# Recurrence steps folded into the input projection, and three re-orderings in the attention loop

## The chip, the cores and the metric

The kernel runs on one core of one Trainium2 chip. The metric is the device time of one execution in microseconds (us). TensorE (PE in the profile) multiplies matrices into the accumulation memory PSUM[...]; VectorE (DVE) and ScalarE (ACT) read and write PSUM and the on-chip memory SBUF; GpSimd (POOL) works on SBUF alone; transfers are issued from the SP and POOL queues. Each engine works through its own instructions in program order and waits on semaphores where it needs another's result. All data here is fp32.

## The reference, cut to what matters

```python
x = L0_attn_x                                   # (2, 2048, 256)
# 1. layernorm, then a tanh recurrence along the sequence, added back
xi = layernorm(x) @ Wi.T + bi
h_t = tanh(xi_t + h_{t-1} @ Wh.T + bh)          # for t in 0..2047, h_{-1} = 0
x = x + h
# 2. layernorm, then attention with experts, added back: 8 heads of 64, 5 experts, 2 of them taken
xn = layernorm(x)
q, k = xn @ Wq, xn @ Wk
gl_v, gl_o = xn @ Ws, xn @ Wd                   # gates, per head and expert
xv = einsum('btd,edk->btek', xn, Wv)            # experts' values
v = einsum('bthe,btek->bhtk', top2(gl_v) * sigmoid(gl_v), xv)
attn = softmax(q @ k.T / 8) @ v
out = x + einsum('bthe,bthk,ekd->btd', top2mask(gl_o), attn, Wo)
```

## The kernel before

**The recurrence.** The sequence of 2048 is cut into 128 pieces of 16 positions; all pieces advance together, so a step is one product with `Wh` over 2 x 128 columns. Since a piece needs the state at the end of the one before it, the recurrence is run twice: run "a" starts every piece from zero at position 3 (`SKIP`) and keeps only the last states (`ends`); run "b" starts from these and keeps all states (`hs`). `compare` (L502) checks that both give the same last states to within 4 x 2^-23; if not, a flag makes the kernel do everything again in a slow form.

The stage ahead of the runs works on 16 chunks `c`. `measure` takes statistics on DVE, `turn_in` (L290) normalizes on POOL and transposes on PE, `project_in` (L301) multiplies by `Wi` (eight PE instructions of 256 columns, an fp32 product being two instructions) and ACT writes `xi` with the bias added. The chunks' order on PE is written out at L322: transposes of chunk c+1, then the product of chunk c. When all sixteen are done, `run("a", ...)` (L375, `step` at L355) follows: each step has per batch four products of 128 columns, an addition of `xi` on DVE and a tanh on ACT.

**The attention.** There are 64 *units*, one for each batch, head and quarter of 512 queries. A unit takes eight score tiles, each of 128 partitions x 2 x 512. The loop at L1154 goes over *steps* T, four for each unit (`U_T`), two score tiles a step. PSUM holds two score tiles (two banks each), two banks for everything else (`misc`), one for the products (tag "o") and one for the sums (tag "d").

A unit is spread over ten steps and more: in four steps its scores are made, ACT copies each tile to SBUF (`stage`, L648) and DVE folds it into a running maximum (`largest`, L653). Then `turn_max`, `reduce_max` and `spread_max` make the row maxima. Five steps after the scores (`LAG` - 1) its tiles have the maximum taken off (`subtract`, L701: the first two tiles of a unit on DVE, the other six on POOL), ACT takes the exponential (L708), PE multiplies by the values (`products`, L711), a DMA on POOL's queue adds tiles in pairs (`fold`, L728), and PE sums them (`sums`). `take` (L751) then takes the products out of bank "o": ACT copies one half, DVE adds the other.

The order on each engine in a step is the program's: at most one `take` and an exponential; scores; `stage`; the table `between`; the two `largest`; the `subtract`s and folds; the table `before`; products; sums; an exponential; the tables `first_behind` and `behind`. Work of other stages (keys and queries of later heads, the second batch's layernorm and gates, experts' values, the output projection `PLACES`) is put into these tables under a step number.

A step in which the first two tiles of a unit have their maximum taken off is called *fresh*; these are the steps with T mod 4 = 1. On DVE a fresh step goes: `largest` of the second tile, `subtract`, `largest` of the first tile, `subtract`. A score tile's banks are free for PE again when both `stage` and `largest` have read them. A unit's last products are made in a fresh step; `take` follows at the head of the step after it (L1158 to L1162), ahead of everything else on ACT.

**The first head.** In steps 0 to 5 `first_experts` (L594) makes the experts' values of the first batch, three chunks a step (16 PE instructions each), using bank "d" for odd chunks and `misc` for even ones. `mix` and `mix_sum` (L613, L626) weigh them with the gates in four parts, on DVE, at the end of steps 3, 5, 6 and 7. The experts' values of the second batch (`experts`, L586) are made during head 5, in steps 81 to 111, two chunks in every four steps; head 8 fetches them from step 120 on. The second batch's layernorm is turned and its logits are made in steps 55 to 89 (`turn_late`, `logits_late`); its gates follow in steps 91 to 121.

Of the kernel before, what the change touches and what calls it, by code (L numbers as in the profile page):

```python
# [14 lines left out]
P = 128  # L15
# [5 lines left out]
def pass_over(  # L21
# [237 lines left out]

    S = NCH  # L260
    NS = P
    NEWTON = 3


# [8 lines left out]

    with tile_pool(name="prep", bufs=3) as pp, tile_pool(
        name="lna", bufs=3
    ) as lnp, tile_pool(name="ps_xi", bufs=3, space=PSUM) as ps_xi, tile_pool(
        name="ps_t", bufs=3, space=PSUM
    ) as ps_t, tc.manual_schedule():
        norm_of, turned = {}, {}

        def measure(c0, n):
            mv = pp.tile([P, n * B, 2], F32, tag=f"mv{n}", name=f"mva{c0}")
            for c in range(c0, c0 + n):
                for b in range(B):
                    stats(lnp, mv[:, (c - c0) * B + b, :], xt[c][:, b, :], f"a{c}_{b}")
            neg, y = scales(lnp, mv, n * B, f"a{c0}")
            for c in range(c0, c0 + n):
                norm_of[c] = neg, y, (c - c0) * B

        def turn_in(c):  # L290
            neg, y, k = norm_of.pop(c)
            xn = pp.tile([P, B, D], F32, tag="xn", bufs=2, name=f"xn{c}")
            tp = ps_t.tile([P, KC, B, P], F32, tag="tp", name=f"tpa{c}")
            for b in range(B):
                normalize(xn[:, b, :], xt[c][:, b, :], neg, y, k + b)
                for kc in range(KC):
                    nc.tensor.transpose(tp[:, kc, b, :], xn[:, b, kc * P : (kc + 1) * P], ident)
            turned[c] = pp.tile([P, KC, B, P], F32, tag="xnT", bufs=2, name=f"xnT{c}")
            nc.scalar.copy(turned[c], tp)

        def project_in(c):  # L301
            xnT = turned.pop(c)
            for mc in range(KC):
                px = ps_xi.tile([P, B, P], F32, tag="px", name=f"px{c}_{mc}")
                for kc in range(KC):
                    nc.tensor.matmul(  # L306
                        px.rearrange("p b n -> p (b n)"),
                        lhsT=wi[:, kc, mc * P : (mc + 1) * P],
                        rhs=xnT[:, kc].rearrange("p b n -> p (b n)"),
                        start=kc == 0,  # L310
                        stop=kc == KC - 1,
                    )
                nc.scalar.activation(xi[:, mc, c], px, AF.Identity, bias=bsum[:, mc : mc + 1])

        groups, c0 = [], 0
        for n in (1, 1, 2, 3, 4, 5):
            groups.append((c0, n))
            c0 += n
        assert c0 == NCH
        measure(*groups.pop(0))  # L320
        nc.vector.tensor_tensor(bsum, bias[:, 0, :], bias[:, 1, :], ALU.add)
        for c in range(NCH):  # L322
            while groups and groups[0][0] <= c + 2:
                measure(*groups.pop(0))
            if c == 0:
                turn_in(0)
            if c < 2:
                project_in(c)
            if c + 1 < NCH:
                turn_in(c + 1)  # L330
            if c >= 2:
                project_in(c)

# [8 lines left out]

    TOL = 4 * 2.0**-23
    GC = NCH // 2
    SKIP = 3
# [6 lines left out]

    def step(nm, s, prev, h, ps_h):  # L355
        for b in range(B):
            if prev is None:
                for mc in range(KC):
                    nc.scalar.activation(h[:, mc, b, :], xi[:, mc, s, b, :], AF.Tanh)
                continue  # L360
            pre = sp.tile([P, KC, NS], F32, tag=f"pre{b}", name=f"pre{nm}_{s}_{b}")
            for mc in range(KC):
                ph = ps_h.tile([P, NS], F32, tag=f"ph{b}_{mc}", name=f"ph{nm}_{s}_{b}_{mc}")
                for kc in range(KC):
                    nc.tensor.matmul(  # L365
                        ph,
                        lhsT=wh[:, kc, mc * P : (mc + 1) * P],
                        rhs=prev(kc, b),
                        start=kc == 0,
                        stop=kc == KC - 1,  # L370
                    )
                nc.vector.tensor_tensor(pre[:, mc, :], ph, xi[:, mc, s, b, :], ALU.add)
                nc.scalar.activation(h[:, mc, b, :], pre[:, mc, :], AF.Tanh)  # L373

    def run(nm, from_zero, keep_states, ps_h, beside=None):  # L375
        prev = None if from_zero else (lambda kc, b: ends[:, kc, b, 0:NS])
        for s in range(SKIP if from_zero else 0, S):
            if keep_states:
                h = hs[:, :, s]
            elif s == S - 1:  # L380
                h = ends[:, :, :, 1:]
            else:
                h = sp.tile([P, KC, B, NS], F32, tag="h", name=f"h{nm}_{s}")
# [132 lines left out]
    with tile_pool(name="ps_h", bufs=1, space=PSUM) as ps_h:  # L516
        if slow:
            nc.gpsimd.memset(hs[:, :, S - 1], 0.0)
            with tc.For_i(0, NS, 1):
                nc.vector.tensor_copy(ends[:, :, :, 1:], hs[:, :, S - 1])  # L520
                run("c", False, True, ps_h)
            for c in range(S):
                turn_back(c, "c")
                add_back(c, nc.gpsimd)
                stats_back(c, "c")
            *_, root_of[0] = roots(mv2[0], GC, "c")
            for c in range(0, GC, 2):
                xn_of[c] = norm_back(c, "c", pool2)
        else:
            with tc.manual_schedule():  # L530
                run("a", True, False, ps_h)
                run("b", False, True, ps_h, beside)
                turn_back(S - 1, "b")
# [60 lines left out]
    def first_experts(c):  # L594
# [4 lines left out]
            xq_of[0, part] = four.tile([P, 4, DH, E], F32, tag=tag, bufs=1 + (tag == "y"), name=f"xf{part}")  # L599
        xq = xq_of[0, part]  # L600

        pv = ps_o.tile([P, E, DH], F32, tag="d", name=f"pvf{c}") if c % 2 else misc([P, E, DH], f"pvf{c}")
        by_quarters(pv.rearrange("p e k -> p (e k)"), 0, c, wv.rearrange("p c e k -> p c (e k)"))
        nc.scalar.copy(xq[:, c % 4], pv.rearrange("p e k -> p k e"))
        if c % 4 == 3:
# [364 lines left out]

    before, between, first_behind, behind = {}, {}, {}, {}

    def at(table, T, f, *a):
        table.setdefault(T, []).append(lambda: f(*a))

# [8 lines left out]
    for i, (b, h) in enumerate(heads):  # L984
# [10 lines left out]
        at(before, T0 + 2, queries, i, 1)  # L995
        for part in range(4):
            if i == 0:
                at(behind, (3, 5, 6, 7)[part], mix, i, part)
                at(behind, (3, 5, 6, 7)[part], mix_sum, i, part)
            else:  # L1000
                T = T0 + U_T * (part - 2) + 2
                at(behind, T - 2, fetch, i, part)
                at(behind, T, mix, i, part)
                at(before, T + 1, mix_sum, i, part)
        if h == H - 3 and b + 1 < B:
            for c in range(NCH):
                T = T0 + c // 2 * U_T + 1
                at(before if c % 2 else behind, T + c % 2, experts, b + 1, c)
    for b in range(1, B):

# [32 lines left out]
    for u, (i, n) in enumerate(units):  # L1043
# [109 lines left out]
    with tc.manual_schedule():  # L1153
        for T in range(NT):  # L1154
            new = (2 * T, 2 * T + 1)
            sub = [t for t in (2 * (T - LAG + 1), 2 * (T - LAG + 1) + 1) if 0 <= t < 2 * NT]
            old = [t for t in (2 * (T - LAG), 2 * (T - LAG) + 1) if 0 <= t < 2 * NT]
            u_old = (T - LAG) // U_T - 1  # L1158
            done = (T - LAG) % U_T == 0 and 0 <= u_old < len(units)
            fresh = sub and sub[0] % HC == 0  # L1160
            if done:
                take(u_old)  # L1162
            if old:
                exponential(old[1])

# [10 lines left out]
            else:  # L1176
# [92 lines left out]
```

## Time and profile before

| | us |
|---|---|
| median of 3 runs | 1552.19 (1551.83 to 1552.85) |
| the profiled execution | 1552.41 |
| its span, first to last instruction | 1550.6 |
| PE busy | 1506.5 (97%) |
| DVE busy | 1301.1 (84%) |
| POOL busy | 1284.3 (83%) |
| ACT busy | 1242.5 (80%) |
| projection stage, first transpose to first recurrence product | 9.1 to 53.1 |
| run "a" | 53.1 to 74.8 |
| run "b" | from 74.8 |
| attention steps 0 to 8 | 121.5 to 187.6 |
| a unit of the middle of the second batch | 20.30 |

The profile is of one execution. Busy times are those in which at least one instruction of the engine was recorded. PE's products overlap each other (a record of 512 columns lasts about 0.6 us while the next group starts 0.43 us after it), so a short wait of PE need not show as idle time; the distance between the starts of records does show it. The granted TensorE clock was 0.999 of full speed. Times with a decimal point in what follows, such as 1326.07, are positions in the span.

### The profile page before, as it was taken

What the parts mean: (1) busy time and instruction counts of PE and PEld (TensorE: products, weight loads), DVE (VectorE), ACT (ScalarE), POOL (GpSimd) and SP (SyncE); (2) the same over time, 40 slices, a digit from 0 to 9 for tenths busy, and PEclk for the clock granted to TensorE, in tenths of its full rate; (3) what the DMA queues carried; (4) which work ended last, traced back from release to release, by engine and by line L of the source; (5) the groups of instructions that cost most, each with busy time, mean ns of one, the idle gap of its engine ahead of it and who ended that gap; (6) DMA issues with size and microseconds to landing.
All of it is one profiled execution on the core that took longest, in us unless ns stands there. A gap on an engine that the chain in (4) does not pass through costs nothing.

```text
span 1550.6 us, 42383 instructions
## 1 busy us (share of the span) xinstructions
PE 1506.5 (97%) x18078; PEld 533.0 (34%) x18078; DVE 1301.1 (84%) x1807; ACT 1242.5 (80%) x1585; POOL 1284.3 (83%) x852
## 2 busy tenths in 40 slices
PE   6999899999999999999999999999999999999997
PEld 5994222222233333333223332222222222222234
DVE  7374899999998888888987778999989999999974
ACT  4674688888888888888887678888888888888872
POOL 3154699999999988999998688899999999999980
PEclk9999999999999999999999999999999999999999
DMA  6021478898888887788797677888888888888965
GB/s 177 1 110 32 116 166 196 188 182 183 181 178 185 185 166 163 169 177 177 165 206 165 166 164 173 173 175 180 176 180 179 175 171 174 174 174 173 208 146 135
DMA packets 87127, 254.52 MB, mean 164 GB/s; under 512 B 11792, under 2 KB 31376, under 8 KB 86928
## 3 DMA queue, kind: packets, MB, share of 16 engines
q0 software_dynamic: 43488, 164.65, 58.0%
q1 hardware_dynamic: 41808, 86.46, 17.0%
q8 instruction: 143, 2.34, 0.6%
q10 hardware_dynamic: 1632, 0.61, 0.2%
q14 instruction: 56, 0.46, 0.1%
HBM read 59.79 MB, written 50.33 MB: 71 GB/s over the span
## 4 chain that ended last, share of the span: by engine, by line
PE 65%; DVE 18%; ACT 7%; issue 5%; DMA 2%; POOL 1%; ACTq 0%; SPq 0%; DVEq 0%; POOLq 0%
PE s L638 22%; PE o L719 18%; DVE m L660 10%; ACT p L650 5%; PE d L740 5%; PE pk L144 3%; PE pq L163 3%; DVE pro L785 3%; PE pz L899 2%; PE phb L365 2%; PE px L306 1%; PE pha L365 1%; DMA p<-p 1%; ACT p L709 1%; PE pv L577 1%
## 5 line engine op out<-in xcount | busy, mean ns | idle before, releaser
L706 POOL TENSOR_TENSOR p<-p,top 128x1024 f32<-128x1024 f32 x378 | 1009.6, 2780 | 26.2 <-ACT top L699 25.9
L650 ACT COPY p<-s 128x1024 f32<-128x1024 f32 x512 | 511.8, 1013 | 143.8 <-issue 59.2
L709 ACT ACTIVATE p<-p 128x1024 f32<-128x1024 f32 x512 | 538.9, 1064 | 49.5 <-DVE p L706 40.5
L638 PE MATMUL s<-q,k 64*32 64x512 f32 x4096 | 501.5, 596 | 4.7 <-ACT p L650 2.4
L638 PE MATMUL s<-qs,k 64*32 64x512 f32 x4096 | 501.5, 596 | 3.4 <-ACT p L650 1.6
L719 PE MATMUL o<-p,v 128*32 128x512 f32 x4096 | 491.6, 597 | 3.2 <-DVE os L756 2.3
L660 DVE TENSOR_TENSOR m<-s,m 128x1024 f32<-128x1024 f32 x320 | 390.9, 1222 | 83.4 <-PE s L638 73.9
L731 POOL DMA_DIRECT2D p<-p x254 | 264.6, 1043 | 94.4 <-issue 40.7
L719 PEld LDWEIGHTS o<-p,v 128*32 128x32 f32 x4096 | 111.8, 109 | 303.8 <-issue 156.6
L638 PEld LDWEIGHTS s<-q,k 64*32 64x32 f32 x4096 | 100.6, 105 | 155.8 <-ACT p L650 59.5
L638 PEld LDWEIGHTS s<-qs,k 64*32 64x32 f32 x4096 | 100.7, 105 | 153.9 <-ACT p L650 58.1
L706 DVE TENSOR_TENSOR p<-p,pt 128x1024 f32<-128x1024 f32 x126 | 152.5, 1210 | 0.0
L740 PE MATMUL d<-p,ones 128*32 128x512 f32 x1032 | 136.8, 592 | 0.7 <-DMA p<-p 0.7
L660 DVE TENSOR_TENSOR m<-s,p 128x1024 f32<-128x1024 f32 x64 | 78.3, 1224 | 47.2 <-ACT p L650 46.2
L785 DVE TENSOR_TENSOR pro<-po,mr 128x1280 f32<-128x1280 f32 (+1 forms) x65 | 95.6, 1471 | 2.6
L622 DVE TENSOR_TENSOR xq<-xq,wp 128x1280 f32<-128x1280 f32 x60 | 89.2, 1487 | 2.1
L628 DVE TENSOR_REDUCE v<-xq 128x256 f32<-128x1280 f32 x60 | 88.5, 1476 | 0.0
L163 PE MATMUL pq<-xn2T,wq 128*32 128x512 f32 x512 | 62.2, 598 | 0.0
L740 PEld LDWEIGHTS d<-p,ones 128*32 128x32 f32 x1032 | 34.1, 110 | 80.2 <-issue 76.9
L144 PE MATMUL pk<-xn2T,wk 128*32 128x512 f32 x512 | 61.5, 598 | 0.0
L835 POOL DMA_DIRECT2D yd<-pro x48 | 60.9, 1268 | 0.0
L400 POOL TENSOR_TENSOR x<-x,hvb 128x512 f32<-128x512 f32 x14 | 17.9, 1275 | 45.8 <-ACT hs L373 34.2
(176 smaller groups left out, 1473.2 us busy)
## 6 DMA issues: line engine op xcount, KB each, us to landing
p<-p POOLq DMA_DIRECT2D x254, 512.0 KB, 5.4
xq<-xvd SPq DMA_DIRECT2D x60, 640.0 KB, 4.6
yd<-pro POOLq DMA_DIRECT2D x48, 640.0 KB, 6.4
qs<-q SPq DMA_DIRECT2D x64, 128.0 KB, 4.4
yd<-pro SPq DMA_DIRECT2D x8, 640.0 KB, 6.3
y<-yd SPq DMA_DIRECT2D x8, 640.0 KB, 6.9
x<-in_x SPq DMA_DIRECT2D x16, 256.0 KB, 6.2
x1d<-x SPq DMA_DIRECT2D x16, 256.0 KB, 2.0
```

The costliest lines, as they stand in the source:

```text
L144: nc.tensor.matmul(pk[at_col : at_col + 32], lhsT=wk[:, kc, h * DH + g : h * DH + g + 32], rhs=xc[:, kc, c0 // 2 : (c0 + HC) // 2, o, :], ...
L163: nc.tensor.matmul(pq[at_col : at_col + 32, :], lhsT=wq[:, kc, h * DH + g : h * DH + g + 32], rhs=xn2T[:, kc, b, n * QB : (n + 1) * QB], s ...
L622: nc.vector.tensor_tensor(xq, xq, wp.unsqueeze(2).to_broadcast([P, 4, DH, E]), ALU.mult)
L638: nc.tensor.matmul(ss[g : g + 32, o, :], lhsT=k_of[i][half, c, g : g + 32], rhs=q_of[i, n][o][half, :], start=True, stop=True, tile_positi ...
L650: nc.scalar.copy(p, ss)
L660: nc.vector.tensor_tensor(m, ss, ring[t - 1] if c == 1 else m, ALU.max)
L706: eng.tensor_tensor(p, p, top.unsqueeze(1).to_broadcast([P, 2, QB]), ALU.subtract)
L709: nc.scalar.activation(ring[t], ring[t], AF.Exp)
L719: nc.tensor.matmul(o_of[u][at_col : at_col + 32, :], lhsT=v_of[i][:, 2 * c + o, g : g + 32], rhs=ring[t][:, o, :], start=c == 0, stop=c == ...
L731: nc.gpsimd.dma_start(out=ring[t], in_=ring.pop(t + 1), accum_op=ALU.add)
L740: nc.tensor.matmul(den_of[u][32 * g : 32 * (g + 1), :], lhsT=ones32, rhs=ring[(t, t1)[g // 2]][:, g % 2, :], start=first, stop=last, tile_ ...
L785: nc.vector.tensor_tensor(dst, po[:, s : s + n, 0:DH].unsqueeze(1).to_broadcast([P, E, n, DH]), mr[:, s : s + n].rearrange("p s e -> p e s ...
```

## The change

1. **Recurrence.** Run "a" is gone. A new function `first_run(c)` is called behind `project_in(c + 1)`: it multiplies the last state by `Wh` onto the same PSUM bank that holds chunk c's projection (no DVE addition), over both batches at once (256 columns), and ACT takes the tanh with the bias from there. The projection's banks go from three to six; the transposes use `misc`.
2. **First head.** `first_experts` rotates over three banks (`misc`, "o", "d"). The four parts of `mix` move from steps 3, 5, 6, 7 to 2, 4, 5, 6, those of `mix_sum` to 2, 4, 6, 8; some are in the table `between`, ahead of `largest`.
3. **Experts.** The second batch's `experts` come eight steps (two units) later, in steps 89 to 118.
4. **Maxima.** In a fresh step that is not in the set `crowded`, both `largest` come ahead of both `subtract`s. `crowded` holds the first 16 steps, the steps of `turn_late`, those of `PLACES` and the third last step.
5. **Take.** `take` moves from the head of the step after a fresh one to the end of the fresh step, behind products and sums and ahead of the exponential of the first tile.

```diff
-        name="lna", bufs=3
-    ) as lnp, tile_pool(name="ps_xi", bufs=3, space=PSUM) as ps_xi, tile_pool(
-        name="ps_t", bufs=3, space=PSUM
-    ) as ps_t, tc.manual_schedule():
+    ) as lnp, tile_pool(name="ps_xi", bufs=6, space=PSUM) as ps_xi, tc.manual_schedule():
...
-            tp = ps_t.tile([P, KC, B, P], F32, tag="tp", name=f"tpa{c}")
+            tp = misc([P, KC, B, P], f"tpa{c}")
...
+        def first_run(c):
+
+            pxs, prev = px_of.pop(c), h_of.pop(c - 1, None)
+            if slow or c < SKIP:
+                return
+            h = ends[:, :, :, 1:]
+            if c < S - 1:
+                h = pp.tile([P, KC, B, NS], F32, tag="h", bufs=2, name=f"ha_{c}")
+            for mc, px in enumerate(pxs):
+                for kc in range(KC if prev is not None else 0):
+                    nc.tensor.matmul(
+                        px,
+                        lhsT=wh[:, kc, mc * P : (mc + 1) * P],
+                        rhs=prev[:, kc],
+                        start=False,
+                        stop=kc == KC - 1,
+                        skip_group_check=True,
+                    )
+                nc.scalar.activation(h[:, mc], px, AF.Tanh, bias=bsum[:, mc : mc + 1])
+            h_of[c] = h
...
             if c >= 2:
                 project_in(c)
+            if c:
+                first_run(c - 1)
+        first_run(NCH - 1)
...
-                run("a", True, False, ps_h)
-                run("b", False, True, ps_h, beside)
+                run("b", ps_h, beside)
...
-        pv = ps_o.tile([P, E, DH], F32, tag="d", name=f"pvf{c}") if c % 2 else misc([P, E, DH], f"pvf{c}")
+        tag = (None, "o", "d")[c % 3]
+        pv = ps_o.tile([P, E, DH], F32, tag=tag, name=f"pvf{c}") if tag else misc([P, E, DH], f"pvf{c}")
...
+    crowded = set(range(4 * U_T))
...
-                at(behind, (3, 5, 6, 7)[part], mix, i, part)
-                at(behind, (3, 5, 6, 7)[part], mix_sum, i, part)
+                at(between if part == 1 else behind, (2, 4, 5, 6)[part], mix, i, part)
+                at(between if part % 2 else behind, (2, 4, 6, 8)[part], mix_sum, i, part)
...
-                T = T0 + c // 2 * U_T + 1
+                T = T0 + c // 2 * U_T + 2 * U_T + 1
                 at(before if c % 2 else behind, T + c % 2, experts, b + 1, c)
...
             at(behind, T + 2, turn_late, b, c)
+            crowded.add(T + 2)
...
             for tab, t, f, o, *more in PLACES:
+                crowded.add(T + t)
...
+    crowded.add(NT - 3)
...
-            u_old = (T - LAG) // U_T - 1
-            done = (T - LAG) % U_T == 0 and 0 <= u_old < len(units)
             fresh = sub and sub[0] % HC == 0
-            if done:
-                take(u_old)
             if old:
                 exponential(old[1])
...
-            if fresh:
+            if fresh and T in crowded:
                 subtract(sub[0])
             if T % U_T:
                 largest(new[0], ss[0])
+            if fresh and T not in crowded:
+                subtract(sub[0])
             if fresh:
                 subtract(sub[1])
...
                 sums(t, t + 2, t % HC == 0, t % HC != 0)
+            if k >= 0 and k % U_T == U_T - 1:
+                take(k // U_T)
             if sub:
                 exponential(sub[0])
```

More of the change, by code (lines that the diff above doesn't have):

```diff
@@ L261, in pass_over @@
     NS = P
+    SKIP = 3
     NEWTON = 3
@@ L275, in pass_over @@
         name="lna", bufs=3
-    ) as lnp, tile_pool(name="ps_xi", bufs=3, space=PSUM) as ps_xi, tile_pool(
-        name="ps_t", bufs=3, space=PSUM
-    ) as ps_t, tc.manual_schedule():
-        norm_of, turned = {}, {}
+    ) as lnp, tile_pool(name="ps_xi", bufs=6, space=PSUM) as ps_xi, tc.manual_schedule():
+        norm_of, turned, px_of, h_of = {}, {}, {}, {}
         def measure(c0, n):
@@ L302, in project_in @@
             xnT = turned.pop(c)
+            px_of[c] = []
             for mc in range(KC):
-                px = ps_xi.tile([P, B, P], F32, tag="px", name=f"px{c}_{mc}")
+                px = ps_xi.tile([P, 512], F32, tag="px", name=f"px{c}_{mc}")[:, : B * P]
                 for kc in range(KC):
                     nc.tensor.matmul(
-                        px.rearrange("p b n -> p (b n)"),
+                        px,
                         lhsT=wi[:, kc, mc * P : (mc + 1) * P],
@@ L312, in project_in @@
                     )
+                px = px.rearrange("p (b n) -> p b n", b=B)
                 nc.scalar.activation(xi[:, mc, c], px, AF.Identity, bias=bsum[:, mc : mc + 1])
+                px_of[c].append(px)
+        def first_run(c):
[8 more added lines that the diff above has]
+                    nc.tensor.matmul(
+                        px,
+                        lhsT=wh[:, kc, mc * P : (mc + 1) * P],
[6 more added lines that the diff above has]
+            h_of[c] = h
         groups, c0 = [], 0
@@ L332, in pass_over @@
                 project_in(c)
+            if c:
+                first_run(c - 1)
+        first_run(NCH - 1)
     TOL = 4 * 2.0**-23
     GC = NCH // 2
-    SKIP = 3
     sp = rw.enter_context(tile_pool(name="step", bufs=3))
@@ L356, in step @@
         for b in range(B):
[L357 to L360, printed above, removed]
             pre = sp.tile([P, KC, NS], F32, tag=f"pre{b}", name=f"pre{nm}_{s}_{b}")
@@ L373, in step, with run @@
                 nc.scalar.activation(h[:, mc, b, :], pre[:, mc, :], AF.Tanh)
[L375 to L383, printed above, removed]
+    def run(nm, ps_h, beside=None):
+        prev = lambda kc, b: ends[:, kc, b, 0:NS]
+        for s in range(S):
+            h = hs[:, :, s]
             step(nm, s, prev, h, ps_h)
@@ L520, in pass_over @@
                 nc.vector.tensor_copy(ends[:, :, :, 1:], hs[:, :, S - 1])
-                run("c", False, True, ps_h)
+                run("c", ps_h)
             for c in range(S):
```

## The prediction

> **What bounds the kernel now.** I read the page first, then stages by window, then single steps in the timeline.
>
> ```profile
> PE 1506.5 (97%) x18078; PEld 533.0 (34%) x18078; DVE 1301.1 (84%) x1807; ACT 1242.5 (80%) x1585; POOL 1284.3 (83%) x852
> L638 PE MATMUL s<-q,k 64*32 64x512 f32 x4096 | 501.5, 596 | 4.7 <-ACT p L650 2.4
> ```
>
> PE is the bound, and its groups show almost no idle time. But a record lasts 0.6 us while groups start 0.43 us apart, so waits below some 0.17 us, and parts of longer ones, are hidden in it; only start distances tell. The timeline of a fresh step of a middle unit and the step behind it:
>
> ```profile
> 1323.71 1.22 DVE L660 TENSOR_TENSOR m<-s,m 128x1024 f32<-128x1024 f32 x1
> 1324.84 1.21 DVE L706 TENSOR_TENSOR p<-p,pt 128x1024 f32<-128x1024 f32 x1
> 1325.97 1.22 DVE L660 TENSOR_TENSOR m<-s,m 128x1024 f32<-128x1024 f32 x1
> 1327.10 1.21 DVE L706 TENSOR_TENSOR p<-p,pt 128x1024 f32<-128x1024 f32 x1
> 1328.34 0.69 DVE L756 TENSOR_TENSOR os<-o,os 64x512 f32<-64x512 f32 x1
> 1329.07 2.56 DVE L660 TENSOR_TENSOR m<-s,m 128x1024 f32<-128x1024 f32 x2
> ...
> 1326.52 0.61 PE L638 MATMUL s<-qs,k 64*32 64x512 f32 x4
> 1327.24 0.63 PE L638 MATMUL s<-qs,k 64*32 64x512 f32 x4
> ```
>
> PE should have begun the second score tile at 1326.52 + 0.43 = 1326.95; it began at 1327.24, just behind the second maximum (1325.97 + 1.22 = 1327.19). This 0.29 us recurs in units 4 to 13 and 37 to 62 (0.21 in 36); otherwise these steps run at PE's pace, 20.30 us a unit.
>
> Then the stages (PE, PEld, DVE, ACT, POOL busy): run "a", the projection's second half, unit 8, a middle unit, units 20 and 28.
>
> ```profile
> 53.11:74.81 21.70, 21.70 (x194) 21.70 (x195) 13.72 (x47) 14.89 (x50) 0.00 (x0) 1.00 0.01 2
> 28.98:53.11 24.13, 23.33 (x127) 20.02 (x125) 7.72 (x37) 16.69 (x35) 9.80 (x18) 1.00 0.00 1
> 304.84:325.15 20.31, 20.23 (x241) 5.82 (x237) 19.51 (x26) 17.65 (x21) 18.77 (x12) 1.00 0.89 183
> 1214.59:1234.89 20.30, 20.23 (x240) 5.81 (x236) 18.36 (x22) 17.64 (x21) 18.74 (x12) 1.00 0.86 174
> 556.06:580.40 24.34, 23.66 (x310) 7.95 (x305) 18.53 (x22) 19.54 (x27) 19.87 (x14) 1.00 0.84 176
> 738.45:758.75 20.30, 20.22 (x240) 5.81 (x236) 18.37 (x22) 17.63 (x21) 20.22 (x17) 1.00 0.79 165
> ```
>
> The projection is already bound by PE, so run "a" can't hide in it. Units 4 to 11, with the late statistics, have DVE full too. And PE's idle records where the first head starts, and in the units around the experts:
>
> ```profile
> 146.66 3.44 PE L577 MATMUL pvf<-wv,xn2T 128*32 128x320 f32 x48 [1.08 <-ACT q L173]
> 169.14 1.28 PE L577 MATMUL pvf<-wv,xn2T 128*32 128x320 f32 x16 [1.62 <-ACT xf L604]
> 180.90 0.63 PE L638 MATMUL s<-q,k 64*32 64x512 f32 x4 [1.30 <-ACT p L650]
> 187.02 0.65 PE L693 MATMUL pt<-ident,mq 128*128 128x128 f32 x4 [1.16 <-DVE mq L684]
> ...
> 788.55 1.06 PE L719 MATMUL o<-p,v 128*32 128x512 f32 x8 [0.87 <-ACT p L709]
> 811.53 1.05 PE L740 MATMUL d<-p,ones 128*32 128x512 f32 x4 [0.75 <-DMA p<-p]
> ```
>
> **1. Recurrence.** Removed: the stretch from the projection's last product (52.3) to run "b" (74.8), 22.5 us, with 192 instructions of 128 columns 0.113 us apart (21.7/192). Added on PE: 12 steps x 8 instructions of 256 columns. The nearest row is the projection's own product, eight such instructions in 1.73 us: 12 x 1.73 = 20.8. The Trainium skill ("TensorE: Matmul & The Clock Gate", Part 3, The mechanism) says that a weight load overlaps matmuls in flight only when its row group differs; these fill all rows, so by it each 0.19 us load would be paid: 96 x (0.216 + 0.19) = 39 us. The row decides: 0.216 us from start to start with loads of 0.19 inside.
>
> The hand-over: a step's product waits for the tanh of the step before, some 0.7 us behind that step's last product (0.47 for `xi` of the same 256 columns, and the ends). PE meanwhile does the next chunk's transposes (0.43) and projection (1.73): hidden. Without this cover it would be 12 x 0.7 = 8.4. ACT has 0.59 + 4 x 0.47 = 2.5 us of work in an iteration of 3.9. Only the last two hand-overs are bare, some 0.3 and 0.5. Sum 20.8 + 0.8 - 22.5 = -0.9, and a POOL wait of about 0.5 before chunk 6 is covered: **-1.4** (range -2 to +7).
>
> **2. First head.** With three banks the third chunk of a step needn't wait for ACT's copy of the first: 1.08 and 1.62 above and 0.47 at 154.73 go, with their hidden parts 3.6 us. From 165.3 to 188.1 DVE works without a pause, and PE waits for it (180.90, 187.02). One `mix` and `mix_sum` pair (3.2 us) leaves this stretch for step 4, behind which DVE waits 5.0 us for scores; another sum now comes behind `reduce_max`. The transfer of step 3's chunks lands in 3 to 4 us, about when step 4's `mix` wants it, so perhaps 0.5 is lost. Followed through, DVE's stretch starts 2 us earlier and is 3.2 shorter; PE reaches step 9 at 182.7 instead of 187.6: **-4.9** (-6.5 to -1.5; the lower end is the banks without the rest).
>
> **3. Experts.** Units 20 and 21 take 24.34 and 24.16 us with `turn_late` and experts together; units 15 to 19, with `turn_late` alone, 21.25: -6.0. Units 28 and 29 (20.30, 20.63) become what 22 to 27 are, 22.12 and 22.51: +3.7. POOL is full in 28 to 31 because gates run there while PE goes at 20.3, and PE then waits (788.55, 811.53 and their neighbours, some 2.3 in all); with experts PE is slower there and POOL keeps up, as in 22 to 27. Queues: the stores move with ACT's copies on SP; the last is issued in step 118, and head 8 fetches from step 120, two steps (10 us) behind a transfer of 3 to 5. Sum **-4.6** (-6 to +1).
>
> **4. Maxima.** The second maximum ends 0.9 us earlier, so the 0.29 goes. Against it: a DVE instruction that doesn't need the one before starts 0.08 us before its end (1324.84 against 1323.71 + 1.22), the maximum behind a maximum 0.10 after. The skill ("VectorE: DVE Perf Modes", The DRAIN you can't avoid) has each operation wait until the pipe is empty, so order would cost nothing; the rows say +0.19 us a unit. It moves the second `subtract`, the addition of `take` and the next maximum from 1329.07 to 1329.26, and ACT's copy behind that to about 1331.57. PE then starts the next scores at 1331.6 instead of 1331.83: 0.23 gained of 0.29. DVE's waits elsewhere in the unit, 0.66 and 0.77, take the 0.19. The first exponential comes 1.1 later, at 1328.3, and its products only at 1329.7. Units 37 to 60: 24 x -0.23, with 36: -5.6. Units 61 and 62 have no keys behind which to hide: +0.4. In units 4 to 11 DVE's waits are only 0.12 in all, so 0.19 - 0.12 = +0.06 each, and in 12 and 13 (roots on DVE) +0.19: +0.9. Sum **-4.3** (-7.5 to +4).
>
> **5. Take.** ACT's copy (0.56) stood where ACT waited 0.73 for the second subtraction; now it stands at 1326.0, where the products have ended (1325.25), and ACT would wait for the later subtraction anyway. Behind it queue both exponentials and the next `stage`; PE waits for these. DVE's addition keeps its place. **0**; if the products were late, ACT would hand on the delay.
>
> Sum: -1.4 - 4.9 - 4.6 - 4.3 = -15.2. The profiled execution took 1552.4, 0.2 from the median: 1552.2 - 15.2 = **1537**.
>
> **Rivals.** *A, the wait moves (22%)*: the DVE chain of part 4 ends in `stage`, which then holds PE as `largest` did; the 24 units give +0.06 to 0.19 instead of -0.23: 1537 + 7 to 10, 1546. For it: unit 8 shows DVE full at the same 20.31. Against: the waits of 0.66 and 0.77. *B, POOL bounds on (10%)*: POOL has 22.4 us of work in units with gates, so moved experts free nothing, and step 4's `mix` waits for its transfer: parts 2 and 3 give half, 1542. *C, the recurrence is laid bare (5%)*: the tanh isn't in time, 12 x 0.7: with half of A, 1549 to 1553, no measurable change. *D, slower (6%)*: `take` holds ACT. Place: the end of every fresh step; it decides once the products end more than 1.9 us later than the 1325.25 seen, for then both exponentials, `stage` and the next products move with them; 0.5 us in each of 62 units is +31: 1568. Against it: no table puts PE work ahead of the products in a fresh step.
>
> **The numbers.** My case (57%) has 1531 to 1543. With A and B the range that keeps all but some 2 in 10 is **1531 to 1548**. Faster by over 0.2% (3.1 us, about what a measurement of this kernel can tell from no change): 57 + 22 + 10 = 89, less a little: 0.88; within: 0.05; slower: 0.07.
>
> **What the profile after would show.** Projection iterations of 3.9 us and run "b" from about 73.4; no pvf wait, step 9 near 181 in all; 21.25 in units 20 and 21; middle units of 20.07 with the second score tile 0.43 behind the first, the two maxima 0.10 apart. Units of 20.3 speak for A; 28 to 31 still waiting for POOL's work for B; products waiting for the tanh for C; `take`'s copy waiting for PE for D. Wrong beyond all of these: if an end state of the folded recurrence differed by over 4 x 2^-23, everything would run twice.

## The result and the profile after

| | before | after |
|---|---|---|
| median of 6 runs (us) | 1552.52 (1551.83 to 1552.98) | 1538.92 (1538.24 to 1540.69) |
| ratio | | 0.9915 [0.9903, 0.9926] |
| the profiled execution | 1552.41 | 1539.07 |
| its span | 1550.6 | 1537.2 |

The change takes 13.6 us off the median and 13.4 off the span. First the page of the kernel after: busy times, and the group of score products (busy, mean ns of one, idle time before them and what ended most of it).

```profile
PE 1496.9 (97%) x17982; PEld 537.8 (35%) x17982; DVE 1290.6 (84%) x1759; ACT 1234.7 (80%) x1559; POOL 1283.8 (84%) x852
L655 PE MATMUL s<-q,k 64*32 64x512 f32 x4096 | 493.7, 595 | 4.8 <-ACT p L667 2.8
```

PE is the bound as before, and its idle time in this row is what it was (4.7). The row can't show the gain in the middle units; the stages do. Busy times by window of the kernel after: the projection from chunk 5 to run "b", unit 8, unit 20, unit 28, a middle unit (columns: window, length, PE, PEld, DVE, ACT, POOL, clock, DMA share, GB/s).

```profile
28.76:73.56 44.80, 44.10 (x223) 38.16 (x221) 7.83 (x37) 28.35 (x59) 9.84 (x18) 1.00 0.00 1
300.34:320.63 20.29, 20.13 (x241) 5.99 (x237) 19.48 (x26) 17.65 (x21) 18.72 (x12) 1.00 0.88 180
552.00:573.25 21.25, 21.25 (x282) 7.00 (x281) 18.52 (x22) 18.35 (x25) 19.87 (x14) 1.00 0.89 186
728.31:750.43 22.12, 22.12 (x272) 6.97 (x268) 18.56 (x22) 18.33 (x23) 21.68 (x17) 1.00 0.83 180
1202.77:1222.87 20.10, 20.06 (x240) 5.98 (x236) 18.46 (x22) 17.64 (x21) 18.72 (x12) 1.00 0.86 174
```

Before, the stretch from chunk 5's projection to the first product of run "b" ran from 28.98 to 74.65, which is 45.67:

```profile
74.65 1.95 PE L365 MATMUL phb<-ends,wh 128*128 128x128 f32 x16
```

(The 74.8 of the table before is where the last record of run "a" ends.) Unit 8 was 20.31 and is 20.29, unit 20 went from 24.34 to 21.25, unit 28 from 20.30 to 22.12, the middle unit from 20.30 to 20.10. PE's records leave no gap in units 20 and 28.

The timeline of the kernel after, a fresh step of a middle unit and the next step's first scores:

```profile
1310.86 2.54 DVE L677 TENSOR_TENSOR m<-s,m 128x1024 f32<-128x1024 f32 x2
1313.32 2.34 DVE L723 TENSOR_TENSOR p<-p,pt 128x1024 f32<-128x1024 f32 x2
1315.69 0.69 DVE L773 TENSOR_TENSOR os<-o,os 64x512 f32<-64x512 f32 x1
1316.42 2.55 DVE L677 TENSOR_TENSOR m<-s,m 128x1024 f32<-128x1024 f32 x2
...
1313.06 0.58 ACT L772 COPY os<-o 64x512 f32<-64x512 f32 x1
1314.56 2.19 ACT L726 ACTIVATE p<-p 128x1024 f32<-128x1024 f32 x2 [0.93 <-DVE p L723]
1316.66 2.07 ACT L667 COPY p<-s 128x1024 f32<-128x1024 f32 x2
...
1313.67 0.61 PE L655 MATMUL s<-qs,k 64*32 64x512 f32 x4
1314.10 0.61 PE L655 MATMUL s<-qs,k 64*32 64x512 f32 x4
1318.78 0.63 PE L655 MATMUL s<-qs,k 64*32 64x512 f32 x4
```

The two maxima now run one behind the other (2.54 for two; one alone takes 1.22, so the second starts 0.10 after the first ends). The second score tile starts at 1314.10, 0.43 behind the group ahead of it: the 0.29 is gone. `take`'s copy (L772) runs at 1313.06, in ACT's wait for the subtractions. From 1314.56 ACT works without a pause through both exponentials and both `stage` copies to 1318.73, and PE's next scores start at 1318.78, just behind: this row of ACT's is what ends the step now.

The first head in the kernel after. Behind the first scores, these are PE's only two waits with a record of idle time in steps 0 to 9:

```profile
156.31 0.65 PE L710 MATMUL pt<-ident,mq 128*128 128x128 f32 x4 [0.78 <-DVE mq L701]
176.24 0.63 PE L655 MATMUL s<-q,k 64*32 64x512 f32 x4 [1.49 <-ACT p L667]
```

No product of experts' values (pvf) waits any more. Added up by the distance between the units' first score products, after less before: start of the attention -1.0; units 0 to 2 (34.45, 24.95, 21.48 become 32.49, 23.25, 19.85) -5.3; unit 3 +1.0; unit 7 +1.0; units 12 and 13 +0.4; 20 and 21 -6.0; 28 to 31 +1.3; 36 to 60 -5.1; 61 and 62 +0.4; the others together -0.2. Before rounding that is -13.4, the difference of the spans.

### The profile page after: what moved, and what is told of

Read it like the earlier page. It is cut to its first block, busy times and chain, and to the rows that moved or that the text cites. A ratio compares the mean times of both kernels' runs of the same rounds, so it can differ in the third digit from the quotient of the medians.

```text
span 1537.2 us, 42101 instructions
## 1 busy us (share of the span) xinstructions
PE 1496.9 (97%) x17982; PEld 537.8 (35%) x17982; DVE 1290.6 (84%) x1759; ACT 1234.7 (80%) x1559; POOL 1283.8 (84%) x852
## 4 chain that ended last, share of the span: by engine, by line
PE 70%; DVE 16%; ACT 6%; issue 4%; DMA 1%; POOL 1%; SPq 0%; DVEq 0%; ACTq 0%; POOLq 0%
PE s L655 24%; PE o L736 20%; DVE m L677 8%; PE d L757 5%; ACT p L667 4%; PE pk L144 3%; DVE p L723 2%; PE pq L163 2%; DVE pro L802 2%; PE pz L916 2%; PE phb L387 2%; PE pt L710 1%; PE px L307 1%; PE pm L696 1%; PE px L328 1%
## 5 line engine op out<-in xcount | busy, mean ns | idle before, releaser
L655 PE MATMUL s<-qs,k 64*32 64x512 f32 x4096 | 493.7, 595 | 5.4 <-ACT p L667 4.3
L655 PE MATMUL s<-q,k 64*32 64x512 f32 x4096 | 493.7, 595 | 4.8 <-ACT p L667 2.8
L655 PEld LDWEIGHTS s<-qs,k 64*32 64x32 f32 x4096 | 104.5, 106 | 149.6 <-ACT p L667 63.2
L655 PEld LDWEIGHTS s<-q,k 64*32 64x32 f32 x4096 | 104.4, 106 | 149.6 <-ACT p L667 61.5
L723 DVE TENSOR_TENSOR p<-p,pt 128x1024 f32<-128x1024 f32 x126 | 148.8, 1212 | 0.0
L394 DVE TENSOR_TENSOR preb<-phb,xi 128x128 f32<-128x128 f32 x64 | 17.9, 290 | 43.9 <-PE phb L387 43.7
```

What stands on the lines that cost most here:

```text
L655: nc.tensor.matmul(ss[g : g + 32, o, :], lhsT=k_of[i][half, c, g : g + 32], rhs=q_of[i, n][o][half, :], start=True, stop=True, tile_positi ...
L723: eng.tensor_tensor(p, p, top.unsqueeze(1).to_broadcast([P, 2, QB]), ALU.subtract)
```

## The experiments

Where a run was timed only once, it is read by its profile; each was measured beside the kernel before on the same chip. For short stretches I use distances from a fixed event, since the start of the attention alone scatters: it came at 120.9 to 122.6 us in kernels that share the old prologue, and at 120.5 to 122.3 in those that share the new one.

Most of this scatter is the clock. In the four profiles of these kernels in which the attention began at 121.8 or later, the granted TensorE clock (the third figure from the end) was 0.50 for some 3.4 us of the projection; in the others it was 1.00. The same stretch in two kernels with the same prologue, where the attention began at 122.3 and at 120.6:

```profile
25.50:28.50 3.00, 3.00 (x10) 2.43 (x10) 2.66 (x15) 1.00 (x3) 0.84 (x2) 0.50 0.16 38
25.50:28.50 3.00, 3.00 (x19) 2.59 (x18) 2.66 (x14) 2.00 (x4) 0.80 (x2) 1.00 0.15 37
```

Without the late four the start is at 120.9 to 121.5 with the old prologue and at 120.5 to 120.6 with the new one.

### The parts one by one

**Part 1 alone.** The kernel before, with the edits of L262 to L400 of the diff (`first_run`, six banks, run "a" gone), and nothing else.

```diff
+            if c:
+                first_run(c - 1)
+        first_run(NCH - 1)
...
-                run("a", True, False, ps_h)
-                run("b", False, True, ps_h, beside)
+                run("b", ps_h, beside)
```

> Part 1 alone, the recurrence folded into the projection. Theory (the work stays on PE and only what lay between the stages goes): run b starts 1.3 us earlier, near 73.5, each projection iteration takes 3.9 us, and the whole is 1.0 to 1.4 us shorter, inside what the times can tell. Rival (run a is hidden beside the projection): some 20 us shorter. Rival (the tanh is not in time): about 8 us longer.

Measured: 1551.54 against 1552.45, ratio 0.9997 [0.9988, 1.0007]. Run "b" starts at 73.64. From chunk 5's projection to run "b" it takes 44.80 us, as in the kernel after; before it was 45.67. So the part is worth 0.9 us in the trace, which is too little for the times to show.

**Part 2 alone.** Three banks and the spread mixing.

```diff
-        pv = ps_o.tile([P, E, DH], F32, tag="d", name=f"pvf{c}") if c % 2 else misc(...)
+        tag = (None, "o", "d")[c % 3]
+        pv = ps_o.tile([P, E, DH], F32, tag=tag, name=f"pvf{c}") if tag else misc(...)
...
-                at(behind, (3, 5, 6, 7)[part], mix, i, part)
-                at(behind, (3, 5, 6, 7)[part], mix_sum, i, part)
+                at(between if part == 1 else behind, (2, 4, 5, 6)[part], mix, i, part)
+                at(between if part % 2 else behind, (2, 4, 6, 8)[part], mix_sum, i, part)
```

> Part 2 alone, three banks and the earlier mixing. Theory (PE waits in steps 2 to 8 go, DVE has one pair of mixing operations less in its full stretch): step 9 comes 5 to 5.5 us earlier, of which 0 to 1.2 is given back in steps 9 to 15; 4 to 5.5 us shorter in all. Rival (DVE bounds steps 5 to 8 anyway): 1.5 us or less.

Measured: 1547.68 against 1552.45, ratio 0.9971 [0.9961, 0.9980]. Steps 0 to 8 take 60.64 us instead of 66.10: -5.46. Unit 3 then takes 21.90 instead of 21.01. The kernel after shows the same, and the timeline there says why: the close of step 12 on DVE waits for POOL.

```profile
201.84 0.19 DVE L795 RECIPROCAL po<-den 128x4 f32<-128x4 f32 x1
203.14 0.18 DVE L798 TENSOR_TENSOR mr<-po,gates_all 128x20 f32<-128x20 f32 x1 [1.11 <-POOL gates_all L251]
```

DVE reaches step 12 some 5 us earlier, but the gates it needs there are the last link of POOL's own work, whose last operation stands in step 12 too. So 0.9 to 1.0 of the 5.5 is given back.

**Three banks alone**, and **the mixing alone** (the second with the two banks of before): each half of the edit above.

> The three banks of part 2 alone, the mixing where it was. Theory (two causes in part 2): the waits of the experts' values on ACT's copies go, some 3.6 us by step 6, but DVE's full stretch keeps its length, so that step 9 comes 3.6 us earlier at most, against 5.5 for the whole part. If the banks are everything, step 9 comes 5.5 us earlier; if DVE bounds from step 5 on, 1.5 or less.

> The earlier mixing of part 2 alone, with the two banks of before. Theory (PE's supply and DVE's stretch each hide the other): the waits for banks, 3 us, stay, and only what DVE held beyond them goes: step 9 comes 1.5 to 3 us earlier, against 1.2 for the banks alone and 5.5 for both. If mixing is the whole of it, 5.5; if the parts add up, 4.3.

Measured from the start of step 0 to the start of step 9:

| | before | banks | mixing | both |
|---|---|---|---|---|
| to step 6 | 48.85 | 45.82 | 49.88 | 45.0 |
| to step 9 | 66.10 | 64.91 | 64.63 | 60.64 |
| gain | | 1.2 | 1.5 | 5.5 |

(One time each: 1552.50 and 1552.78.) The banks alone are 3.0 us ahead at step 6, and lose 1.8 of it in steps 6 to 8, where DVE has all its mixing and PE waits for it. The mixing alone leaves PE waiting for the banks, and comes to step 6 a microsecond late. Two limits follow each other here, PE's banks and DVE's load, and taking away one hands most of the gain to the other.

**Part 3 alone.** The experts' values of the second batch two units later.

```diff
-                T = T0 + c // 2 * U_T + 1
+                T = T0 + c // 2 * U_T + 2 * U_T + 1
```

> Part 3 alone, the experts' values two units later. Theory (excess of crowded units 20 and 21 goes, 6.0; units 28 and 29 get 3.7 longer; POOL's backlog in units 30 and 31 goes, 2.3): 4.6 us shorter, with units 20, 21 at 21.25 and 28, 29 at 22.1 and 22.5. Rival (POOL's backlog stays): units 30 and 31 still together 44 us, 2.3 us shorter in all.

Measured: 1547.81 against 1552.45, ratio 0.9974 [0.9962, 0.9985]; units 30 and 31 at 20.30 and 21.55 (before 21.42, 22.59). The work moved costs 3.7 us in units 28 and 29 where it saved 6.0 in 20 and 21, and PE's recorded waits in 30 and 31 (0.87 and 0.75) go. So moving the experts does free something, and the explanation that POOL stays the bound there falls.

**Part 4 alone.** Both maxima ahead of the subtractions, `take` still at the head of the next step.

```diff
-            if fresh:
+            if fresh and T in crowded:
                 subtract(sub[0])
             if T % U_T:
                 largest(new[0], ss[0])
+            if fresh and T not in crowded:
+                subtract(sub[0])
```

> Part 4 alone, both maxima ahead of the subtractions, with take left at the head of the next step. Theory of the record (take's place is worth nothing): middle units of 20.10 us, about 3.4 us shorter in all. New theory (the two belong together: with the first subtraction 1.3 us later, ACT does the first exponential, then take's copy, then the second exponential without a pause, so DVE's addition and the copy of the next scores come 0.4 to 0.5 us later): middle units of 20.4 to 20.6 us, about 6 to 10 us longer in all.

Measured: 1564.48 against 1552.45, ratio 1.0082 [1.0065, 1.0099]: 12 us slower, more than the 6 to 10 of the new theory. Middle units take 20.52 (units 36 to 60 add 5.5 us in all), units 4 to 13 some 0.2 to 0.75 more than before (4.9 in all), 61 and 62 20.52 instead of 19.91 (1.2). First ACT in the kernel before, from the start of a fresh step's scores (1326.07):

```profile
1326.08 1.06 ACT L709 ACTIVATE p<-p 128x1024 f32<-128x1024 f32 x1
1327.05 0.56 ACT L755 COPY os<-o 64x512 f32<-64x512 f32 x1
1328.35 1.06 ACT L709 ACTIVATE p<-p 128x1024 f32<-128x1024 f32 x1 [0.73 <-DVE p L706]
```

`take`'s copy (L755) ends 0.73 before the second subtraction does, so it costs nothing. Then the timeline of this kernel; the fresh step's scores start at 1335.06:

```profile
1336.41 1.06 ACT L709 ACTIVATE p<-p 128x1024 f32<-128x1024 f32 x1 [1.40 <-DVE p L706]
1337.37 0.56 ACT L755 COPY os<-o 64x512 f32<-64x512 f32 x1
1337.84 1.05 ACT L709 ACTIVATE p<-p 128x1024 f32<-128x1024 f32 x1
1339.99 1.01 ACT L650 COPY p<-s 128x1024 f32<-128x1024 f32 x1 [0.21 <-ACT p L650]
...
1337.97 0.69 DVE L756 TENSOR_TENSOR os<-o,os 64x512 f32<-64x512 f32 x1 [0.46 <-ACT os L755]
1338.69 2.55 DVE L660 TENSOR_TENSOR m<-s,m 128x1024 f32<-128x1024 f32 x2
...
1341.06 0.63 PE L638 MATMUL s<-qs,k 64*32 64x512 f32 x4 [0.42 <-ACT p L650]
```

Because of the reordering the first exponential starts 1.3 us later in the step, directly behind the delayed subtraction. `take`'s copy is queued behind it on ACT (1337.37) and holds up the second exponential and both `stage` copies by 0.47 us; DVE's addition waits for the copy, and PE waits for the `stage`. From this step's first scores to the next it is 6.00 us here, 5.77 before and 5.57 in the kernel after.

**Part 5 alone**, and **parts 4 and 5 together.** `take` at the end of the fresh step:

```diff
-            if done:
-                take(u_old)
...
+            if k >= 0 and k % U_T == U_T - 1:
+                take(k // U_T)
             if sub:
                 exponential(sub[0])
```

> Part 5 alone: take at the end of the fresh step, maxima in the old order. Both theories: worth nothing by itself, since ACT's copy goes into time that ACT waits for the second subtraction anyway; middle units stay at 20.30 us, the whole within 1 us of before. If take held up ACT (rival D of the prediction), middle units would be longer than 20.30.

> Parts 4 and 5 together, nothing else. Theory (they belong together): middle units of 20.10 us, where part 4 alone gave 20.52 and part 5 alone gives 20.30; units 12, 13 and 61, 62 some 0.2 us longer each than before; 3 to 4.5 us shorter in all. If the two were independent, the pair would be as much longer as part 4 alone, 12 us.

Measured: part 5 alone 1552.63 against 1552.76, ratio 1.0000 [0.9991, 1.0009], units of 20.30: nothing. Both: 1551.30 against 1552.76, ratio 0.9992 [0.9982, 1.0001], middle units of 20.10. So the one part costs 12 us, the other gives nothing, and the two together some 1.5, which is less than the 3 to 4.5 expected and by the interval not clear of no change: `take` is worth about 13 us behind part 4 and nothing without it. The middle units show the same without the scatter of the times: 20.30, +0.22, 0.00, and -0.20 for the pair. That the pair gives less than 24 x 0.20 = 4.8 is unit 7 (21.71 instead of 20.31), which comes next; units 11 to 13, 61 and 62 (+1.0 together); units 30 and 31 (22.03 and 22.76, +0.8, with experts where they were); and +1.2 behind the start of the last unit, a stretch that took anything from 72.1 to 74.0 us in these profiles.

### What the new order costs where it doesn't help

The wait of 0.29 was in units 4 to 13, 61 and 62 as well (the second score tile starts 0.72 instead of 0.43 behind the group ahead of it), and the new order removes it there too. But there PE is not what sets the length. In unit 61 the scores of the fresh step and of the next one start, before and then after:

```profile
1447.90 0.63 PE L638 MATMUL s<-qs,k 64*32 64x512 f32 x4
1453.27 0.63 PE L638 MATMUL s<-qs,k 64*32 64x512 f32 x4 [0.42 <-ACT p L650]
```

```profile
1433.82 0.63 PE L655 MATMUL s<-qs,k 64*32 64x512 f32 x4
1439.38 0.63 PE L655 MATMUL s<-qs,k 64*32 64x512 f32 x4 [0.33 <-ACT p L667]
```

This step has no product for later keys, so PE waits for `stage` in both kernels, and with the new order `stage` ends 0.19 later: 5.37 us become 5.56, the length that this step has in the middle units too. In units 8 to 10 the fresh step gains its 0.20 (5.77 to 5.57) and the step ahead of it loses 0.16 (4.61 to 4.77); in unit 12 the last step loses 0.41 (5.38 to 5.79). DVE is nearly full there (19.5 of 20.3 us in unit 8), but these two losses were not followed to one instruction.

In the kernel after unit 7 takes 21.34. Its close on DVE waits for the store of the unit before:

```profile
285.13 0.18 DVE L798 TENSOR_TENSOR mr<-po,gates_all 128x20 f32<-128x20 f32 x1
286.41 1.49 DVE L802 TENSOR_TENSOR pro<-po,mr 128x1280 f32<-128x1280 f32 x1 [1.10 <-DMA yd<-pro]
```

With the new order the queues reach that store later: two transfers of queries ahead of it on SP go about 0.4 us later, the store is issued 0.6 us later and lands 8.2 us after its issue (5.1 before). Why it takes longer to land is not shown. If the order is the cause, unit 7 must fall back to 20.3 when it alone is undone there. Two kernels undo it in the stretches where a unit gains nothing (4 to 13, 61, 62), by this edit to the kernel after:

```diff
-    crowded = set(range(4 * U_T))
+    crowded = set(range(14 * U_T)) | {61 * U_T + 1, 62 * U_T + 1}
```

The second of them is this edit alone. The first also makes the gates of the first head's part 0 one step earlier, comparisons and all, against the wait in unit 3:

```diff
-        at(behind, 7 + 6 * part, gates, 0, part, 1, False)
+        at(behind, 6 + 7 * part, gates, 0, part, 1, False)
...
-            at(behind, 8 + 6 * part + k, gates_go_on)
+            at(behind, 7 + 7 * part + k, gates_go_on)
```

> The changed kernel with two edits. The old order of maxima also in steps 17 to 53 and in 245 and 249, where the new one cost 0.2 us a unit or gained nothing: units 11 to 13 and 61, 62 shorter by 0.1 to 0.2 us each, unit 7 back to 20.3 if its wait for a store was brought on by the order. And the first head's output gates one step earlier, so that they are ready for the first close in step 12: unit 3 back from 22.0 to about 21.0. Together 1.5 to 3 us shorter than the changed kernel; if the wait in unit 3 has another cause, 0.5 to 2.

> The changed kernel with the old order of maxima also in steps 17 to 53 and in 245 and 249, nothing else. From the run before this: units 4 to 13 back to 20.3 to 21.2, 61 and 62 back to 19.91, unit 3 still 22.0; 1.5 to 2 us shorter than the changed kernel, near 1537. If unit 7's wait for a store is chance, 0.8.

Measured: the order alone 1537.65, ratio 0.9906 [0.9889, 0.9922] to the kernel before. Unit 7 falls to 20.30, units 12 and 13 to 21.10 and 21.19, 61 and 62 to 19.90 and 19.91. With the gates moved: 1540.55, ratio 0.9921 [0.9908, 0.9935]. Unit 3 is back at 21.0, but step 9 comes 64.84 us after step 0 instead of 60.64. This kernel's timeline in step 7, up to the first scores of step 8:

```profile
173.82 1.09 DVE L240 TENSOR_TENSOR lt<-lg,gates_all 128x256 f32<-128x256 f32 x4 [1.52 <-ACT lg L227]
...
180.16 0.63 PE L655 MATMUL s<-q,k 64*32 64x512 f32 x4 [4.11 <-ACT p L667]
```

The gates begin with comparisons on DVE that need a copy from ACT; put a step earlier they keep DVE idle for 1.52 us and then busy for 1.09, just where it is full, and PE waits 4.11. In the kernel after PE waits 1.49 at this place, so 2.6 us come from here. The rest is the clock: behind this wait the granted clock is 0.50 for some 3.4 us,

```profile
181.00:184.00 3.00, 3.00 (x28) 0.99 (x12) 0.18 (x1) 2.65 (x4) 2.71 (x3) 0.50 0.30 60
```

and step 8 takes 6.48 us instead of 4.90. A wait of 1 us was traded for 4.2.

**The last of POOL's gate operations alone, a step earlier**, with the order above:

```diff
-            at(behind, 8 + 6 * part + k, gates_go_on)
+            at(behind, 8 + 6 * part + min(k, 3 + part), gates_go_on)
```

> As the run beside it, and the last operation on the first head's output gates moved from step 12 to step 11 (the comparisons stay where they were). Theory (unit 3 is longer because the first close waits 1.1 us for POOL's last operation on the gates): unit 3 near 21.0 and another 1 us shorter, near 1536. Rival (POOL is full there and only the order changes): unit 3 stays at 22.0 or POOL's subtractions are late and step 12 or 13 is longer.

Measured: 1537.16 (1536.17 to 1537.93), ratio 0.9898 [0.9881, 0.9914]. Unit 3 takes 20.99, and step 12's close no longer waits:

```profile
203.63 0.19 DVE L795 RECIPROCAL po<-den 128x4 f32<-128x4 f32 x1
203.92 0.18 DVE L798 TENSOR_TENSOR mr<-po,gates_all 128x20 f32<-128x20 f32 x1
```

So the wait of 1.11 was POOL's last operation and nothing else. From the start of step 0 to the end of the span it is 1416.7 us in the kernel after, 1415.1 with the order undone in those units, 1413.8 with this as well (of these last 1.3 us, 0.9 is unit 3 and 0.5 lies behind the start of the last unit, where the profiles scatter). This version has the lowest median of all. The medians go the same way, but the intervals of the last two overlap with that of the kernel after, so that these 1 to 2 us are shown by the units of the profiles and not by the times.

### The price of a bare hand-over

Does other work on PE really hide the recurrence's wait for tanh? In this kernel (part 1 alone otherwise) two steps of the recurrence come in a row after every second chunk, so that in each pair the second has nothing to hide behind:

```diff
-            if c:
+            if c % 2 == 0 and c:
+                first_run(c - 2)
                 first_run(c - 1)
+        first_run(NCH - 2)
         first_run(NCH - 1)
```

(The last two steps are again a pair.)

> Part 1 with two recurrence steps one behind the other after every second chunk, so that one hand-over in two has no transposes and projection ahead of it. Theory (the cover is what makes part 1 free; a bare hand-over costs 0.3 to 0.5 us, as the last one does): five or six bare hand-overs, run b starts 1.5 to 3 us later than with part 1 as it is. If the tanh were fast enough anyway, no later.

The timeline of this kernel, and below it that of the kernel after:

```profile
66.89 4.02 PE L328 MATMUL px<-ha,wh 128*128 128x256 f32 x16
70.74 1.89 PE L307 MATMUL px<-xnT,wi 128*128 128x256 f32 x8
72.47 4.02 PE L328 MATMUL px<-ha,wh 128*128 128x256 f32 x16
77.06 1.16 PE L389 MATMUL phb<-ends,wh 128*128 128x128 f32 x8 [0.57 <-ACT ends L336]
```

```profile
65.52 1.89 PE L328 MATMUL px<-ha,wh 128*128 128x256 f32 x8
67.25 1.89 PE L307 MATMUL px<-xnT,wi 128*128 128x256 f32 x8
68.98 4.02 PE L328 MATMUL px<-ha,wh 128*128 128x256 f32 x16
73.56 1.60 PE L387 MATMUL phb<-ends,wh 128*128 128x128 f32 x12 [0.56 <-ACT ends L336]
```

A single step takes 1.89 and starts 1.73 before the next group; two without a break would be 1.89 + 1.73 = 3.62, and a pair takes 4.02. A bare hand-over costs 0.40. From chunk 5's projection to run "b" it takes 46.81 us against 44.80, +2.0, which is five more pairs at 0.40. (Run "b" starts at 77.06 against 73.64 with part 1 as it is; the other 1.4 came ahead of chunk 5, where the edit changes nothing but this execution had the granted clock at 0.50 for some 3.4 us. The one time was 1554.55.) In the kernel after only the last pair and the ends are bare.

## Why the prediction was right, and where not

The time came to 1538.9 where 1537 was forecast, and the case taken for likeliest is the one that happened: no new bound took over in the middle units, which carry the gain. Against the steps:

| | predicted | measured in the kernel after |
|---|---|---|
| 1. recurrence | -1.4 | -0.9 up to run "b" |
| 2. first head | -4.9 | -5.5 in steps 0 to 8, +1.0 in unit 3 |
| 3. experts | -4.6 | -4.7 |
| 4. maxima (with 5) | -4.3 | -3.3 |
| 5. take | 0 | 0 alone, about -13 behind part 4 |

**Recurrence.** The 0.216 us from product to product held: iterations of 3.89 against 3.9. The rule of the Trainium skill that was weighed against it ("TensorE: Matmul & The Clock Gate", Part 3, The mechanism) would have made 39 us of the 20.8. One sentence of the section allows only a different row group; another names a background weight buffer beside it as a target of a load that is pulled ahead. The rows go against the first and fit the second, though no run here shows which buffer a load used. The cover by projection was right, and the bare hand-over costs 0.40, below the 0.7 that the rival used; the rival with the recurrence laid bare would have lost 12 x 0.40 = 4.8 us, not 8.4. (Its own sum, 1537 + 8.4 and half of A's 7 to 10, comes to 1549 to 1550, not to 1553.) The missing 0.5 is two small terms: the two bare hand-overs cost 0.40 and 0.72 instead of 0.3 and 0.5, and the wait before chunk 6 that is covered now was 0.26 (31.40 - 28.98 = 2.42 from projection to projection, where the next ones take 2.16), not 0.5.

**First head.** The estimate of the gain up to step 9 was 0.6 short. What the step didn't see is the consumer at the other end: POOL's gates were on time for the old start of step 12 and not for one 5 us earlier.

**Experts.** Units 20 and 21 (21.25 each), 28 and 29 (22.12, 22.50) and the waits in 30 and 31 came as worked out. Rival B, that POOL bounds on, fell.

**Maxima.** The middle units gained 0.20 of the 0.23 forecast, 36 the same, and 61 and 62 lost 0.19 to 0.20 as forecast; 12 and 13 lost 0.20 and 0.19, as forecast; units 4 to 10, where +0.06 each was forecast, lost nothing apart from unit 7, and unit 11 lost the 0.06. The swap costs DVE what the two gaps said (-0.08 and +0.10), though the general form of the step, that an instruction which doesn't need the one before starts 0.08 before its end, is too wide: in the lines shown there, `take`'s addition starts 0.03 after the end of a subtraction that it doesn't need. The first rival, that the wait moves, came true in part, in units 4 to 13, 61 and 62. The 1.0 of unit 7 was in no step: it is a store that comes late through SP's queue.

**Take.** This is the step that failed: "and ACT would wait for the later subtraction anyway" prices `take` at **0** and leaves the whole gain to part 4. It was followed through only in its new place. In its old place, behind part 4's later subtraction, the copy stands between the two exponentials and costs 0.42 us in a middle unit (20.52 against 20.10). The sum came right because both were made together, which is luck as far as this step goes; had only part 4 been made, the forecast would have been some 17 us too low (1552.2 - 4.3 = 1547.9, measured 1564.5). The last rival named the right mechanism, ACT's queue handing on a delay, but at the wrong edit: moving `take` cures it and not moving it brings it on.

## What to carry to other kernels

When an instruction on one engine is moved later, look at what stands in the next engine's queue behind its consumer: an unrelated copy that used to fall into a wait can end up in the path, and moving it may be worth more than the edit itself. Price coupled edits as a pair, and ask of each stage that gets earlier which other engine's result it will now meet too soon. A wait removed pays only where the engine that waited sets the pace: the 0.29 went in all the units, which gained 0.20 in the middle ones, cost 0.19 to 0.20 where another engine's row was as long, and 1.0 in one where the new order delayed a store. So apply a reorder in the stretches where it pays. And before a difference of a microsecond is put down to an edit, compare the granted clock of the two executions.

## What the hardware showed that I had not expected

- Order alone matters on DVE: two subtractions and two maxima take 0.19 us longer if the maxima come together. In the kernel after a maximum starts 0.10 us after the end of a maximum just ahead of it (114 pairs), and a subtraction 0.08 before the end of a maximum just ahead of it (79 pairs). That the maxima depend on each other is a likely reason, but not a shown one: of the other pairs, `pro` starts 0.03 after the end of `mr`, which it needs (64 pairs), and `take`'s addition 0.03 after the end of a subtraction, which it doesn't (62 pairs). The section of the Trainium skill cited in the prediction ("VectorE: DVE Perf Modes", The DRAIN you can't avoid) says of the wait for an empty pipe also that an operation which isn't held starts earlier, so that it allows for the 0.08.
- One and the same store (`yd` from `pro`) took 5.1, 6.8 and 8.2 us from issue to landing, in the kernel before, with the order undone and in the kernel after. The transfers ahead of it on SP come in the same order in all three; it is issued 18.8, 18.8 and 19.3 us behind the start of unit 6.
- In five of the fourteen profiles the granted clock was 0.50 for some 3.4 us while the projection ran, and in one of them again behind a wait of 4.11 us ahead of step 8. Where two executions can be compared closely, such a spell delays what follows by 1.2 to 1.7 us. That is as large as part 1's whole effect, and hides it in a single time. What sets it off in one execution and not in another is not shown.
